# A two-layer transformer kernel: four stages in a row become one pipeline over blocks of 512 queries

## The chip, the cores and the metric

The kernel runs on one core of one Trainium2 chip. The core has a matrix engine (TensorE, PE in the profile; its weight loads are shown as PEld), a vector engine (VectorE, DVE), an activation engine (ScalarE, ACT), a general engine (GpSimd, POOL), and SyncE (SP), which here only issues transfers. Each of them works through its own list of instructions in order. Matrix products are written to PSUM, 8 banks of 512 float32 numbers on each of 128 partitions; everything else lies in SBUF, on 128 partitions, or in DRAM.

The metric is the device time of the whole program in microseconds (us), inputs to output. Three runs are given, and the median counts. The profile is of one further execution.

## The reference, cut to what matters

One sequence of 4,096 tokens with 256 channels goes through two layers, each a modulated norm, a mixer over tokens and a mixer over channels, all in float32 but for the last product.

```python
# sa..gb: six rows of 256 from silu(c) @ wmod; ga, gb pushed away from zero
h = layernorm(x) * (1 + ca) + sa
x = x + ga * attention(h)          # 16 heads of 16, causal softmax; keys gated
h = layernorm(x) * (1 + cb) + sb
x = x + gb * mixture(h)            # shared SwiGLU + 8 experts, the best 2 of a token
# second layer, with its own six rows
h = layernorm(x) * (1 + ca) + sa
x = x + ga * delta_rule(h)         # short convolutions, rotary, chunks of 32, a scan
h = layernorm(x) * (1 + cb) + sb
x = x + gb * quantised(h)          # rounded to int8, 256 x 256 product, rescaled

# attention: out = (softmax(q k / 4, causal) * gate[key]) @ v
#   gate = tanh(g2(gelu(g1(drift)))), drift from a small network on h
# mixture:   wdense = softmax(h @ w_gate) where among the best 2, else 0
#   out = swiglu(h @ w_in) @ w_out + sum_e wdense[:, e] * (swiglu(h @ w1) @ w2[e])
# delta rule, per head and chunk of 32 tokens, k and q normed, beta and gamma gates:
#   T = (I + strict_lower(beta k k'))^-1;  u = T (beta v);  w = T (beta k)
#   u_t = u - w S;  o = q S + tril(q k') u_t;  S = mean(gamma) S + k' u_t
#   core = rmsnorm(o) @ Wo;  plus gate * rmsnorm(sum of dilated shifts of h)
```

Two properties set the order of the work: the attention of a block of 512 queries needs the keys and values of that block and of the earlier ones, none of later ones; and the scan's state S goes through all 128 chunks in order. Mixture, convolutions and the last product work token by token, or look back by at most 8 tokens.

## The kernel before, in words

The kernel runs four stages one after the other, each with its own pools of buffers and banks, each over 8 blocks of 512 tokens.

**Inputs** (`setup`, then `attn_inputs`, from L361): the modulation rows, then for each block the norm (statistics on DVE, the power -1/2 on POOL at L109, the application on DVE at L125), transposes on PE, the products with the weights of k, q and v, and the gate's small network. k and q are stored to DRAM (`kd`, `qd`) as a high and a low half, with rows doubled, so that one product of 48 rows gives the logits at full precision. Values stay in SBUF (`vall`) for all 32 tiles of 128 tokens, multiplied by the gate at the end of the stage.

**Attention** (`interleave`, `maxima`, `weighted`, `divided`): 32 steps, four groups of 4 heads outermost and the 8 query blocks inside, up and down in turn. A step at block T consists of 4T + 3 units: 4T keys tiles before the block, and three for the triangle. For each unit PE makes the logits of 128 keys by 512 queries for 4 heads, as two pairs of heads; the products of a pair lie on different rows of the array, and follow each other with nothing between. Each of those products fills a bank `e` (three banks in turn), and ACT takes the exponential from it at L586. Then PE multiplies by the values into a bank `o`. I call the work with one pair of heads a half-unit; there are 1,088 of them.

The softmax needs its maximum beforehand. `maxima` makes the same logits a second time, the queries in rows: a pair of heads fills a double bank `m` of 1,024 columns (two such in turn), and one DVE reduction over 128 x 2 x 512 takes both maxima, at L479. The negated maximum is stored, as two halves, into two more rows of the query tile by a transfer, so that the product of 50 rows gives logits minus maximum. `maxima` runs up to 4 steps ahead of `weighted`, at a rate worked out from what is due. The full keys of a group (`kts`, 4,096 columns) lie in SBUF in two sets, so that a group's keys are loaded once.

**Mixture** (`mixture`, L626 to L764): per block the output projection, the norm, the choice of experts, two SwiGLU products, and for each tile the shared product and eight experts; DVE adds the experts' products, weighted, into `acc` (L760). All weights lie in SBUF.

**Layer 1** (`layer1`, with two streams, `fronts` and `backs`): the front of a block is its norm, the products for q, k, v, the short convolutions as products with diagonal matrices (`convolve`), transposes (`by_channel`), the products k k' (`products`), and the triangular `solve`, 31 columns of two DVE instructions each (L1194, L1201), whose result goes through DRAM into `U`. The back of a tile is `from_inverse` (u and w), the `scan` of four chunks (PE L146 into bank `w`, DVE `ut` at L1271, PE again, DVE state `S` at L1293), then `weights`, `outputs`, `projected`, and for each block `quantised`. The front runs some 7 pieces ahead; a piece of back and 14/15 of a piece of front follow each other. Four banks `f` serve both.

The order on PE is the order in which the program writes these pieces (`keep_in_program_order` in `mm` and `tp`); DVE's order in layer 1 is fixed for the solve and the scan (`inturn`).

Of the kernel before, what the change touches and what calls it, by code (L numbers as in the profile page):

```python
# [15 lines left out]
PSUM = bass.MemoryType.PSUM  # L16

P = 128
S = 4096
C = 256  # L20
NT = S // P
NB = S // 512
MASKED = -1e30
LN_EPS = 1e-5
V_N = 16 * 17 + 15
AHEAD = 4
HIGH = -4096
ROUND = 12582912.0

K_ID = 0
K_ONE = K_ID + P
K_RANK = K_ONE + 1
K_N = K_RANK + 8
C_QK = 0
C_KQ = C_QK + P
C_N = C_KQ + P
D_INC = 0
D_CH = D_INC + P  # L40
D_EYE = D_CH + 4
D_N = D_EYE + 16 * 32
LEAD = 7
RATE = 14 / 15
KEPT = 8


def _constants():
    import numpy as np

    i = np.arange(P)
    a, b = i[:, None], i[None, :]
    chunk = (a // 32) == (b // 32)

    k = np.zeros((P, K_N), np.float32)
    k[:, K_ID : K_ID + P] = np.eye(P)
    k[:, K_ONE] = (i % 32) == 16
    k[:, K_RANK : K_RANK + 8] = 8 - np.arange(8)
    causal = np.zeros((P, C_N), np.float32)
    causal[:, C_QK : C_QK + P] = np.where(b > a, MASKED, 0.0)  # L60
    causal[:, C_KQ : C_KQ + P] = np.where(a > b, MASKED, 0.0)
    delta = np.zeros((P, D_N), np.float32)
    delta[:, D_INC : D_INC + P] = chunk & (a <= b)
    delta[:, D_CH : D_CH + 4] = ((i[:, None] // 32) == np.arange(4)[None, :]) / 32.0
    eye = np.eye(32, dtype=np.float32)
    for e in range(2):
        delta[64 * e : 64 * e + 64, D_EYE:] = eye[e::2].reshape(1, -1)

    f = np.float32
    freq = f(1.0) / f(10000.0) ** (np.arange(0, 64, 2, dtype=f) / f(64))  # L70
    ang = np.arange(S, dtype=f)[:, None] * freq[None, :]
    trig = np.concatenate([np.cos(ang), np.sin(ang)], axis=1).astype(f)
    return {"const_k": k, "const_causal": causal, "const_delta": delta, "const_trig": trig}


class _Net:
    def __init__(self, ctx, tc, a, out):
        self.ctx, self.tc, self.nc, self.a, self.out = ctx, tc, tc.nc, a, out
        self.n = 0

# [6 lines left out]

    def rows(self, pool, vec, n, tag):

# [5 lines left out]

# [5 lines left out]

# [4 lines left out]
    def power(self, pool, src, n, tag):  # L106

        r = self.t(pool, [P, n], tag)
# [3 lines left out]
    def normed(self, pool, srcs, width, tag):  # L112

        nc = self.nc
        st = self.t(pool, [P, 4, 6], tag + "st")
        mv = self.t(pool, [P, 4, 2], tag + "mv")
# [3 lines left out]
        ve = self.t(pool, [P, 4], tag + "ve")  # L120
        nc.vector.tensor_scalar(ve, mv[:, :, 1], LN_EPS, None, ALU.add)
        rs = self.power(pool, ve, 4, tag + "rs")
        xn = self.t(pool, [P, 4, width], tag + "xn")
        for s in range(4):
            nc.vector.tensor_scalar(  # L125
                xn[:, s, :], srcs[s], mv[:, s, 0:1], rs[:, s : s + 1], ALU.subtract, ALU.mult
# [3 lines left out]
    def transposed(self, psum, tag, src, outs, scale, bias):  # L130

        nc = self.nc
        for k in range(2):
            ps = self.t(psum, [P, 512], tag)
            for s in range(4):
                nc.tensor.transpose(
                    ps[:, s * P : (s + 1) * P], src[:, s, k * P : (k + 1) * P], self.ident
                )
            nc.scalar.activation(
                outs[k], ps, AF.Identity, bias=bias[:, k : k + 1], scale=scale[:, k : k + 1]  # L140
            )

    def mm(self, out, lhsT, rhs, start=True, skip=False):

        self.tc.keep_in_program_order(
            self.nc.tensor.matmul(out, lhsT, rhs, start=start, stop=True, skip_group_check=skip)  # L146
        )
# [3 lines left out]
    def setup(self):  # L151
        nc, a = self.nc, self.a
        self.const = cp = self.ctx.enter_context(self.tc.tile_pool(name="const", bufs=1))
# [6 lines left out]
        nc.vector.memset(self.mhalf, -0.5)  # L160

        with self.tc.tile_pool(name="modw", bufs=2) as wp, self.tc.tile_pool(
            name="modp", bufs=2, space=PSUM
        ) as pp:
            self.mods = [self.modulation(i, wp, pp) for i in range(2)]

    def modulation(self, layer, wp, pp):
# [11 lines left out]

        ps = self.t(pp, [P, 8], "pc")  # L180
        for n, part in enumerate((0, 1, 3, 4)):
            for ch in range(2):
                for k in range(2):
                    nc.tensor.matmul(
# [3 lines left out]
                        start=(k == 0),  # L188
                        stop=(k == 1),
# [3 lines left out]
        for n, name in ((2, "ca"), (6, "cb")):  # L193
            nc.vector.tensor_scalar(col[:, n : n + 2], col[:, n : n + 2], 1.0, None, ALU.add)
        m["sa"], m["ca"], m["sb"], m["cb"] = (col[:, 2 * n : 2 * n + 2] for n in range(4))


        for part, name in ((2, "ga"), (5, "gb"), (3, "sbr"), (4, "cbr")):
# [3 lines left out]
            for k in range(2):  # L202
                nc.tensor.matmul(
                    pr, scb[:, k, :], wm[:, k, part * C : (part + 1) * C], start=(k == 0), stop=(k == 1)
                )
            row = self.t(cp, [P, C], f"{name}{layer}")
# [16 lines left out]

    def attention(self):
        nc, tc, a = self.nc, self.tc, self.a  # L230
        ap_ = self.ctx_attn
        self.vall = self.t(ap_, [P, NT, V_N], "vall")
        self.kts = [[self.t(ap_, [P, S], f"kt{i}{p}", F32R) for p in range(2)] for i in range(2)]
        for pair in self.kts:
            for kt in pair:
                nc.gpsimd.memset(kt.bitcast(F32), 1.0)
        nc.gpsimd.memset(self.vall, 1.0)
        dp = self.ctx.enter_context(tc.tile_pool(name="halves", bufs=1, space=bass.MemoryType.DRAM))
        self.kd = self.t(dp, [3 * C, S], "kd")
        self.qd = self.t(dp, [3 * C, S], "qd")  # L240
        self.attn_inputs()

        wp = ap_
        causal = self.t(wp, [P, C_N], "causal", BF16)
        nc.gpsimd.dma_start(out=causal, in_=a["const_causal"])
        self.masks = []
        for at in (C_QK, C_KQ):
            four = self.t(wp, [P, 4, P], f"mask{at}", BF16)
            nc.vector.tensor_copy(four, causal[:, at : at + P].unsqueeze(1).to_broadcast([P, 4, P]))
            self.masks.append(four)  # L250

        self.mxs = [self.t(wp, [P, 4, 4, 2 + NB], f"mx{i}") for i in range(2)]
        for m in self.mxs:
            nc.gpsimd.memset(m, MASKED)

        with ExitStack() as c:
            e = c.enter_context
            self.qp = e(tc.tile_pool(name="q", bufs=AHEAD))
            self.pexp = e(tc.tile_pool(name="pexp", bufs=10))
            self.small = e(tc.tile_pool(name="asmall", bufs=2))  # L260
            self.ps_e = e(tc.tile_pool(name="ps_e", bufs=3, space=PSUM))
            self.ps_m = e(tc.tile_pool(name="ps_m", bufs=2, space=PSUM))
            self.ps_o = e(tc.tile_pool(name="ps_o", bufs=1, space=PSUM))


            self.interleave([(g, T if g % 2 == 0 else NB - 1 - T) for g in range(4) for T in range(NB)])

    def interleave(self, steps):


        halves = [2 * (4 * T + 3) for _, T in steps]
        start = [sum(halves[:k]) for k in range(len(steps) + 1)]

        order = []
        for k in range(len(steps)):
            order += [(k, False)] * 3 + ([(k - 1, True)] if k else []) + [(k, False)] * (halves[k] - 3)
        order.append((len(steps) - 1, True))
        need = [order.index((k, True)) + 1 for k in range(len(steps))]
        first = [order.index((k, False)) for k in range(len(steps))] + [len(order)]
        streams = {}  # L280
        self.q, done, due = {}, 0, 0.0

        def ahead(upto):
            nonlocal done
            while done < upto:
                k, _ = order[done]
                if k not in streams:
                    streams[k] = self.maxima(*steps[k], k)
                next(streams[k], None)
                done += 1  # L290

        self.load_keys(1)
        for k in range(AHEAD):
            self.load_queries(*steps[k])
        ahead(need[0])
        due, values, tail = float(done), None, None
        for i, (g, T) in enumerate(steps):
            if i and i + AHEAD - 1 < len(steps):
                self.load_queries(*steps[i + AHEAD - 1])
            if i in (9, 17):  # L300
                self.load_keys(g + 1)
            ahead(need[i])
            due = max(due, done)
            limit = first[min(i + AHEAD, len(steps))]
            main = self.weighted(g, T)
            for n in range(halves[i] // 2):
                for half in range(2):
                    made = next(main)
                    at = start[i] + 2 * n + half + 1
                    rates = [  # L310
                        (need[k] - due) / max(start[k] - 4 - at, 1)
                        for k in range(i + 1, min(i + AHEAD, len(steps)))
                    ]
                    due = min(due + max([0.0, *rates]), limit)
# [450 lines left out]

# [700 lines left out]
```

## Time and profile before

| | us |
|---|---|
| three runs | 3,789.13, 3,801.37, 3,807.05 |
| median | 3,801.37 |
| the profiled execution, span | 3,803.7 |
| inputs, from the start to the first weighted unit | 0 to 283 |
| attention | 283 to 2,080 |
| mixture | 2,080 to 2,621 |
| layer 1 | 2,621 to 3,804 |
| busy over the span: PE, PEld | 3,167.0, 1,744.3 |
| busy over the span: DVE, ACT, POOL | 2,234.4, 1,521.2, 451.5 |
| transfers | 88.45 MB, HBM read 51.05, written 33.55 |

The profile gives no time of the execution beside its span. A digit in the 40 slices is the busy share of 95 us in tenths. "Idle before" is how long an engine stood still just ahead of a group's instructions, and the arrow names what ended most of that. A group is one line of the kernel, one operation and one pair of tiles with their shapes (partitions x elements); "x" counts them, and the mean is in ns. A matmul's shape is given as rows of the array by columns of it, then the moving operand; busy matmuls can overlap, so the busy time of PE is that of the union.

### The profile page before, as it was taken

The numbers are of one execution on the slowest core, as the hardware profiler recorded it, in microseconds if no ns is written. First come the engines' busy times: TensorE is split into PE (matmuls) and PEld (weight loads), VectorE is DVE, ScalarE is ACT, GpSimd is POOL, SyncE is SP. The second block draws the span as 40 slices with busy tenths as digits, with TensorE's granted clock in tenths as the row PEclk, the third lists the DMA queues.
The fourth block names the chain that finished last, engine by engine and source line by source line (L and its number), as shares of the span: only waits on it lengthen the run. The fifth ranks groups of instructions, "written<-read, shape, count | busy, mean of one in ns | idle before, by whom it ended". The sixth has DMA issues, their size and how long they took to land. (4 is left out here: it accounts for less than half of the span.)

```text
span 3803.7 us, 52206 instructions
## 1 busy us (share of the span) xinstructions
PE 3167.0 (83%) x20876; PEld 1744.3 (46%) x20876; DVE 2234.4 (59%) x4101; ACT 1521.2 (40%) x3022; POOL 451.5 (12%) x564
## 2 busy tenths in 40 slices
PE   5768899999999899999998898987876887787765
PEld 3444333333334333333334444443755666665644
DVE  4326887877656887877763343444546555554554
ACT  1213565677765565677776111111322122122111
POOL 4230000000000000000000112121312122222211
PEclk7775998999998998999999898987877788878855
DMA  4450000020002000000001100000000000100000
GB/s 131 146 162 10 10 5 5 5 39 5 10 10 52 10 10 5 5 5 5 5 10 40 46 0 1 0 0 23 11 16 14 18 13 14 20 11 15 16 16 12
DMA packets 142563, 88.45 MB, mean 23 GB/s; under 512 B 102448, under 2 KB 120368, under 8 KB 141744
## 3 DMA queue, kind: packets, MB, share of 16 engines
q1 hardware_dynamic: 142176, 85.04, 8.7%
q8 instruction: 165, 2.70, 0.3%
q14 instruction: 78, 0.64, 0.1%
q0 software_dynamic: 144, 0.07, 0.0%
HBM read 51.05 MB, written 33.55 MB: 22 GB/s over the span
## 5 line engine op out<-in xcount | busy, mean ns | idle before, releaser
L479 DVE TENSOR_REDUCE mx<-m 128x2 f32<-128x1024 f32 (+3 forms) x1088 | 1191.4, 1129 | 400.4 <-PE m L146 398.9
L586 ACT ACTIVATE e<-e 128x512 f32<-128x512 f32 (+1 forms) x2176 | 1108.4, 588 | 616.9 <-PE e L146 612.5
L146 PE MATMUL e<-q,kt 50*128 50x512 f32 (+3 forms) x2688 | 731.8, 427 | 106.8 <-ACT e L586 101.4
L146 PEld LDWEIGHTS e<-q,kt 50*128 50x128 f32 x2688 | 326.1, 190 | 749.6 <-ACT e L586 617.9
L146 PE MATMUL m<-kt,q 48*128 48x512 f32 (+2 forms) x2688 | 599.1, 405 | 51.0 <-DVE mx L479 23.5
L146 PE MATMUL o<-e,vall 128*32 128x512 f32 (+3 forms) x5376 | 593.8, 533 | 0.0
L146 PEld LDWEIGHTS m<-kt,q 48*128 48x128 f32 x2688 | 290.1, 198 | 132.4 <-DVE mx L479 64.2
L977 PE MATMUL f<-conv,pT 128*128 128x128 f32 x1536 | 242.9, 313 | 0.0
L667 POOL TENSOR_TENSOR y<-y,ga 128x512 f32<-128x512 f32 x16 | 20.2, 1263 | 1816.1 <-DMA w1s<-in_L_ffn_w_shared_dram 1804.2
L751 PE MATMUL p<-w,hid 128*128 128x512 f32 x512 | 225.0, 592 | 0.0
L977 PEld LDWEIGHTS f<-conv,pT 128*128 128x128 f32 x1536 | 216.1, 220 | 14.2 <-issue 7.0
L146 PEld LDWEIGHTS o<-e,vall 128*32 128x32 f32 x5376 | 118.6, 111 | 172.5 <-issue 167.2
L760 DVE SCALAR_TENSOR_TENSOR acc<-p,wd,acc 128x256 f32<-128x256 f32 x256 | 123.9, 484 | 125.4 <-PE p L751 120.9
L751 PEld LDWEIGHTS p<-w,hid 128*128 128x128 f32 x512 | 97.3, 190 | 108.8 <-issue 107.1
L146 PE MATMUL w<-S,uw 64*32 64x64 f32 x1024 | 64.0, 256 | 97.3 <-DVE S L1293 96.7
L1293 DVE TENSOR_TENSOR S<-gs,w 128x128 f32<-128x128 f32 x128 | 36.3, 283 | 175.5 <-PE w L146 174.6
L487 DVE TENSOR_REDUCE mx<-m 128x8 f32<-128x1024 f32 x64 | 78.5, 1226 | 76.9 <-PE m L146 76.1
L146 PE MATMUL f<-v,U 128*128 128x64 f32 x256 | 45.3, 336 | 68.0 <-DMA U<-dU 67.9
L146 PEld LDWEIGHTS w<-S,uw 64*32 64x32 f32 x1024 | 39.4, 125 | 135.7 <-DVE S L1293 108.7
L977 PE MATMUL f<-frac,hT 128*128 128x128 f32 x640 | 91.2, 297 | 0.0
L747 ACT COPY acc<-p 128x256 f32<-128x256 f32 x32 | 11.9, 373 | 192.9 <-PE p L743 192.9
L977 PEld LDWEIGHTS f<-frac,hT 128*128 128x128 f32 x640 | 84.1, 208 | 3.4 <-issue 0.3
(266 smaller groups left out, 3559.9 us busy)
## 6 DMA issues: line engine op xcount, KB each, us to landing
kd<-half SPq DMA_DIRECT2D x48, 256.0 KB
qd<-half SPq DMA_DIRECT2D x48, 256.0 KB
q<-qd SPq DMA_DIRECT2D x128, 96.0 KB
kt<-kd SPq DMA_DIRECT2D x12, 768.0 KB
x<-in_L_attn_x_dram SPq DMA_DIRECT2D x16, 512.0 KB
Ls<-dL SPq DMA_DIRECT2D x64, 64.0 KB
out_dram<-x SPq DMA_DIRECT2D x8, 512.0 KB
wm<-in_L_wmod_dram SPq DMA_DIRECT2D x2, 1536.0 KB
```

The lines of the kernel that those rows point to most:

```text
L146: self.nc.tensor.matmul(out, lhsT, rhs, start=start, stop=True, skip_group_check=skip)
L479: nc.vector.tensor_reduce(mx[:, 2 * pair : 2 * pair + 2, s, col], ps[:, :, at : at + w], AX.X, ALU.max)
L487: nc.vector.tensor_reduce(mx[:, 2 * pair : 2 * pair + 2, :, 0], ps.rearrange("p h (s k) -> p h s k", k=P), AX.X, ALU.max,)
L586: nc.scalar.activation(e[:, 0:width], ps[:, 0:width], AF.Exp)
L667: nc.gpsimd.tensor_tensor(y, y, m["ga"].unsqueeze(1).to_broadcast([P, 2, C]), ALU.mult)
L747: nc.scalar.copy(acc, ps)
L751: nc.tensor.matmul(ps, hid[1][:, k, rows], w2[:, k, 2 * ep : 2 * ep + 2, :], start=(k == 0), stop=(k == 1),)
L760: nc.vector.scalar_tensor_tensor(acc, ps[:, e2, :], wd[:, s, ei : ei + 1], acc, ALU.mult, ALU.add)
L977: self.nc.tensor.matmul(out, lhsT, rhs, start=(k == 0), stop=(k == n - 1))
L1293: nc.vector.tensor_tensor(self.state, gs, pw[:, 0, 128:256].rearrange("p (a d) -> p a d", d=64), ALU.add)
```

## The change

The four stages become one loop over steps of the attention, now with the query blocks outermost and ascending and the four head groups inside, so that a block's heads are complete after four steps. Three streams run together:

- `attention` gives the order. For each half-unit it makes an e pair, yields a place for one piece of "back" (scan and what follows it), makes the previous unit's values product, makes the next step's maxima, and after every second of these yields a place for one piece of "front". The maxima run one step ahead.
- `fronts` is, in order: the inputs of blocks 0 and 1, the weights of layer 1, then for each block b the inputs of b + 2, and once block b's heads are complete its mixture and its layer 1 front. `step` lets the front advance as long as the PE time that its pieces have taken (estimated in `mm`) is below a due amount, 150 us per 74 units.
- `backs` is the scan and what follows, for 32 tiles.

What is left after the last unit is done in `drain`.

Buffers change with it. PSUM: 2 banks e, 2 single banks m, 1 o, 1 f for the fronts, and one double bank g for the backs; before the first and after the last unit (`solo`) the fronts also use e and m. A pair of maxima products fills two banks m, and two DVE reductions of 128 x 512 take the place of one of 1,024. SBUF: chunks of 512 keys come from DRAM into rings of two, one ring for e and one for m, and values likewise; the heads go to DRAM (`od`) and come back; the weights of the mixture, of q, k, v and of inputs are loaded again for each block. `scr` holds everything short-lived in three sizes, 6 buffers each.

Work is moved between engines, too. `folded` multiplies Wo, the shared output weights and the experts' by ga and gb/2 at the start (on POOL, and stored to DRAM), in place of multiplying results. Silu and sigmoid are written with tanh, with one more DVE operation. The norms are applied on ACT instead of DVE. The solve's 496 instructions go to POOL from DVE; beta is multiplied into L on ACT and into U on POOL, so the transposes of beta k are gone. DVE adds the experts' products straight into x.

```diff
     def attention(self):
+        steps = [(g, T) for T in range(NB) for g in range(G)]
...
+            main = self.weighted(k, steps)
...
+            for n in range(n_units):
+                for half in range(2):
+                    value = next(main)
+                    yield "back", units
+                    if half == 0 and values is not None:
+                        done, values = values(), None
...
+                    want = min(n_max, round(n_max * (2 * n + half + 1) / max(2 * n_units - 3, 1)))
+                    while made < want:
+                        next(ahead, None)
+                        made += 1
+                        if made % 2 == 0 or made == want:
+                            yield "front", units
...
+    def run(self):
+        self.setup()
+        self.resident()
...
+        while self.ready < 1:
+            next(front)
+        self.front, self.back = front, back
+        for kind, units in self.attention():
+            self.step(kind, units)
+        self.solo = True
+        self.drain()
+
+    def step(self, kind, units):
+        if kind == "back":
...
+                self.at = self.advance_back()
+            return
+        due = (units - FIRST) / PER_BLOCK * FRONT_PE
+        if self.spent < due:
+            before = self.pe
+            if next(self.front, self) is self:
+                return
+            self.spent += self.pe - before
...
+            for tag, n in (("e", 2), ("m", 2), ("o", 1), ("f", 1), ("g", 1))
...
     def maxima
-            ps = self.t(self.ps_m, [P, 2, 512], "m")
+            pss = [self.t(self.banks["m"], [P, B], "m") for _ in range(2)]
...
+                    for par, ps in enumerate(pss):
+                        nc.vector.tensor_reduce(mx[:, 2 * pair + par, s, 2 + ch : 3 + ch], ps, AX.X, ALU.max)
...
+    def load_keys(self, z, g, ch):
+        tiles = self.keys[z]
+        kt = tiles[self.loaded[z] % 2]
+        for par in range(2):
+            self.nc.sync.dma_start(
+                out=kt[64 * par : 64 * par + 48].bitcast(F32),
+                in_=self.kd[ch].rearrange("(a b) r n -> b r a n", b=2)[par][:, 2 * g : 2 * g + 2],
+            )
+        v = None
+        if z == "e":
+            v = self.vals[self.loaded[z] % 2]
+            self.nc.sync.dma_start(
+                out=v[:, :, 0:V_N], in_=self.vd[ch][g].rearrange("(j p) n -> p j n", p=P)
+            )
...
     def solve(self, b, later):
-                    nc.vector.tensor_tensor(
+                nc.gpsimd.tensor_tensor(
                     step[:, 0:m, 0:n],
...
-                self.inturn(nc.vector.tensor_tensor(below, below, step[:, 0:m, 0:n], ALU.subtract))
+                nc.gpsimd.tensor_tensor(below, below, step[:, 0:m, 0:n], ALU.subtract)
...
+    def normed(self, srcs, width, tag):
+        rs, nm = self.statistics(srcs, tag)
+        xn = self.scratch([P, 4, width], tag + "xn")
+        for s in range(4):
+            self.nc.scalar.activation(
+                xn[:, s, :], srcs[s], AF.Identity, bias=nm[:, s : s + 1], scale=rs[:, s : s + 1]
+            )
+        return xn
...
+        for src, dst, row in [
+            (a["L0_attn_Wo"], self.wo_d, m["ga"]),
+            (a["L0_ffn_w_shared_out"], self.wso_d, half),
+        ] + [(a["L0_ffn_w2"][i], self.w2_d[i], half) for i in range(8)]:
+            w = self.weight(wp, src, C, "fold")
+            nc.gpsimd.tensor_tensor(w, w, row.unsqueeze(1).to_broadcast([P, 2, C]), ALU.mult)
+            nc.sync.dma_start(out=dst.rearrange("(k p) n -> p k n", p=P), in_=w)
...
+                th = self.scratch([P, B], "th")
+                nc.scalar.activation(th, pa, AF.Tanh, scale=0.5)
+                nc.vector.scalar_tensor_tensor(hh[:, hc, :], th, 1.0, pa, ALU.add, ALU.mult)
...
+    def load_inverse(self, n):
...
+        self.nc.gpsimd.tensor_tensor(
+            U, U, self.tiles[n]["beta"].unsqueeze(2).to_broadcast([P, 4, P]), ALU.mult
+        )
```

## The prediction

> **What bounds the kernel now.** I read the page's totals first, then a table by stretches cut at the four stages, then the attention's waits, groups and timeline, then the last 200 us.
>
> The page, engines and the 40 slices (tenths of a slice busy; PEclk is the granted clock):
> ```profile
> span 3803.7 us, 52206 instructions
> PE 3167.0 (83%) x20876; PEld 1744.3 (46%) x20876; DVE 2234.4 (59%) x4101; ACT 1521.2 (40%) x3022; POOL 451.5 (12%) x564
> ...
> PE   5768899999999899999998898987876887787765
> DVE  4326887877656887877763343444546555554554
> ...
> PEclk7775998999998998999999898987877788878855
> ```
> The stretches: inputs, attention, mixture, layer 1, and layer 1's last part (length, then busy time of PE, weight loads, DVE, ACT, POOL, then the granted clock):
> ```profile
> 0.00:283.00 283.00, 187.74 (x664) 121.09 (x664) 98.73 (x333) 49.99 (x69) 94.62 (x92) 0.75 0.46 147
> 283.00:2080.00 1797.00, 1635.63 (x11376) 673.60 (x11376) 1303.31 (x1308) 1139.14 (x2241) 0.00 (x0) 0.95 0.05 11
> 2080.00:2621.00 541.00, 464.31 (x1281) 248.79 (x1280) 213.72 (x564) 72.29 (x119) 94.64 (x107) 0.88 0.05 15
> 2621.00:3610.00 989.00, 764.65 (x6482) 615.25 (x6483) 519.57 (x1626) 237.03 (x542) 229.88 (x336) 0.81 0.09 16
> 3610.00:3804.00 194.00, 114.70 (x1076) 85.56 (x1074) 99.11 (x273) 22.73 (x52) 32.37 (x31) 0.54 0.06 14
> ```
> PE is the busiest engine of every stage: 66%, 91%, 86%, 77% and 59%. The attention's 161 idle us are few, but the other stages leave 95, 77, 224 and 79 us idle, at lower clocks. So the upper limit of what an overlap can bring is about 640 us of idle PE plus the clock, less what must stay alone at both ends.
>
> Inside the attention, its groups and its waits (busy us, mean ns | idle before it; then who waited for whom, us, times, longest):
> ```profile
> L479 DVE TENSOR_REDUCE mx<-m 128x2 f32<-128x1024 f32 x896 | 1069.3, 1224 | 359.2 <-PE m L146 357.7
> L146 PE MATMUL e<-q,kt 50*128 50x512 f32 x1792 | 613.6, 484 | 92.6 <-ACT e L586 91.3
> L146 PE MATMUL m<-kt,q 48*128 48x512 f32 x1792 | 489.0, 446 | 28.3 <-DVE mx L479 23.5
> ```
> ```profile
> PE e L146 <- ACT e L586: 102.2, 396, 0.5
> ```
> Equal numbers of equal matmuls cost 613.6 us for e and 489.0 for m. The timeline of one unit shows why: with three e banks the second pair of a unit is split, each half running alone after a wait for an exp, where an m pair runs as two in 0.4 to 0.5 us.
> ```profile
> 1801.97 0.50 PE L146 MATMUL e<-q,kt 50*128 50x512 f32 x2
> 1802.31 0.40 PE L146 MATMUL m<-kt,q 48*128 48x512 f32 x2
> 1802.55 0.40 PE L146 MATMUL e<-q,kt 50*128 50x512 f32 x1
> 1803.15 0.50 PE L146 MATMUL e<-q,kt 50*128 50x512 f32 x1 [0.21 <-ACT e L586]
> ```
>
> **The sum is made against the profiled execution**, 3,803.7 us of span with no other time of its own shown; the median of the three runs is 3,801.4, so I treat the two as one. Runs differ by 0.5% (3,789 to 3,807): less than that is "the same", about what a measurement of this kernel can tell from no change.
>
> **The change, part by part.** The new run has three pieces: a head up to the first attention, a pipelined stretch, and a tail for the last block.
>
> *Pipelined stretch, work on PE.* The matmuls stay, but for half of the transposes f<-k,kk (22.2 us), 11. All PE work is then 3,167 - 11 = 3,156. Outside the stretch lie the setup's 25 and one block's inputs (163/8 = 20), and at the end one block's mixture (464/8 = 58), its layer 1 (879/8 = 110) and a third of the scan part of the block before (its rows sum to about 49 a block: 17), by the order in which the changed program's PE instructions stand. That leaves 3,156 - 45 - 185 = 2,926.
>
> *Pairs of e.* Two e banks take the place of three, but between one e pair and the next now stand an m pair, often an o group, and one of 904 inserted pieces of other work of 0.2 to 2.9 us each by their rows. Two exps take 1.2 us (601 ns each). I take e at m's price: -125. Ends: -125 and 0.
>
> *Clock.* The 1,290 us of other work in the stretch ran at 0.75, 0.88 and 0.81 (0.83 weighted); the attention at 0.95. At 0.95 they would take 1,122, a gain of 168; ends 0 and 168. I take 110, because much of layer 1 is small matmuls that keep PE thin wherever they stand. PE work: 2,926 - 125 - 110 = 2,691.
> [...]
>
> *New waits.* The maxima lose their double banks: a pair of m matmuls fills both m banks, and the next pair must wait until both have been reduced. A 128x512 reduce is 685 ns (the row 128x2 from 128x512), so two take 1.37 us where one of 1,024 took 1.22; that adds 0.15 x 896, 130 us in all, to DVE, and the smaller ones some 80. The scan's solve goes to POOL, the apply of three norms to ACT; the tanh forms and fused sums come to DVE. By rows DVE has about 1,500 us of maxima and 850 of other work, 2,370 in all. The stretch has 1,088 half-units (one e pair each): PE 2,691/1,088 = 2.47 us, DVE 1.37 plus (850 - 100)/1,088 = 0.69, 2.06. DVE is below PE, but its queue is in order: the bursts of the convolution's rotation (two of 0.71, two of 0.55, four of 0.35) and its waits for POOL's power (1.0 us) stand between reduces, and behind them the m pair and everything after it on PE. Today PE waits 102 for ACT and 47 for DVE, 0.14 us per half-unit; the other end is that all of DVE's other work shows, 0.69. I take 0.30, nearer to today's since the pieces are spread one to a half-unit: 326 us. The single banks f and g of the inserted work are in it: the next user stands a half-unit or more later, except in two runs of 19 and 21 us for whole inputs.
>
> *The DMA queue.* SP issues 1,667 transfers instead of 816, at 0.3 to 0.56 us, 0.7 ms of its own time, and keys and values are read again for each step: 288 pairs of key loads and 144 of values, some 130 MB. Today's 85 MB took 8.7% of the engines, so about 22%. A chunk is asked for a whole chunk ahead, four units or about 22 us; a 512 KB load issued at 2,089.8 was used at 2,096.9, 7 us later. I cost it at nothing. Were half the chunks 3 us late, it would be 430 us.
>
> *Solve on POOL.* 496 instructions at 0.25 to 0.53 us (the POOL row cs of 128x128 is 530 ns) are 125 to 260 us that the pipeline hides, seven times in eight. POOL and DVE can hold each other up, as these three rows of the last stretch show, where the second of two equal adds takes 3.25 instead of 1.22 us:
> ```profile
> 3715.95 1.22 DVE L1382 TENSOR_TENSOR yxn<-yxn,cbr 128x1024 f32<-128x1024 f32 x1
> 3715.99 3.38 POOL L1396 TENSOR_TENSOR x<-x,bgo 128x1024 f32<-128x1024 f32 x1 [2.38 <-ACT yxn L951]
> 3717.20 3.25 DVE L1383 TENSOR_TENSOR yxn<-yxn,sbr 128x1024 f32<-128x1024 f32 x1
> ```
> POOL did nothing in the whole attention, so no row shows whether reduces suffer too; if each of 250 us of solve held up a reduce, that would be 250 more.
> [...]
>
> *Head.* The first axn stands at 53.7 us today. Before it now come ten weights loaded, multiplied (1.27 us on POOL) and stored through two buffers, five rounds of about 8 us, and the building of 34 diagonal weights on POOL (0.35 us, 12); then the block's chain to its values, 35, and the maxima of the first step. I take 125, ends 95 and 160. The 283 us of today fall away in exchange.
>
> *Tail.* After the last attention unit: a mixture alone, 75 (2,079 to 2,155 today for the first block); layer 1's front for four tiles, 85 (2,650 to 2,735 today); the solve on POOL, 30; from the end of the solve at 3,653.6 to the end today, 150. Sum 340, ends 300 and 390.
>
> **Sum**: 125 + 2,691 + 326 + 340 = 3,482: 3,480 us, 8.5% faster.
>
> **Rivals.** (a) *No better work on PE*: e stays split and the clock low, since two e banks split pairs as three do. 125 + 2,926 + 326 + 340 = 3,717. For it: ACT must return two banks rather than one and a half. Against it: 2.47 us between pairs for 1.2 us of exps.
> (b) *Slower: m pairs wait for DVE.* With one pair of banks PE stands before each m pair until DVE has worked off what stood in front of its reduces. At 0.69 us per half-unit: 125 + 2,691 + 750 + 340 = 3,906. It decides from 0.60 us on, (3,804 - 3,156)/1,088. For it: the tight 2.06 against 2.47 us. Against it: bursts come about 32 times for the convolutions, not 1,088 times.
> (c) *Full overlap*: waits stay at today's 0.14 and the clock reaches 0.95: 125 + 2,633 + 152 + 340 = 3,250.
> That the stages do not overlap at all is excluded by the order on PE: no inserted run but two is over 3.6 us.
>
> **How the numbers follow.** Likeliest (3,330 to 3,640) 50%; (a) and mixtures towards it, up to 3,785, 18%; within 0.5% of before 4%; (b), above 3,823, 24%, since the room on DVE that decides it, 0.41 us a half-unit, is less than one burst; (c) 4%. Faster 0.72, same 0.04, slower 0.24. The range 3,300 to 3,920 takes in (b)'s 3,906, the end of the largest unknown cost, and leaves about 4% below and 10% above.
>
> **What would show it.** Right: PE at 87% or more from 130 us to the last attention unit, granted clock 0.9 or better there, e's busy time near m's, no mixture or layer stretch but the last 340 us, DVE near 2,370 us busy. Wrong: PE waits on mx above 650 us in sum; e or m waiting on key loads; a tail over 400 us; DVE's reduces longer than 0.7 us beside POOL.

## The result, and the profile after

The changed kernel takes 4,580.33 us (median of four runs, 4,568.1 to 4,581.6) against 3,804.21 us (the three runs of before and one more): 1.205 times as long, interval 1.201 to 1.209. The forecast was 3,480 us, faster.

The page of the changed kernel, engines and slices:
```profile
span 4566.3 us, 55163 instructions
PE 3844.8 (84%) x20812; PEld 1912.4 (42%) x20812; DVE 2177.4 (48%) x4732; ACT 1586.6 (35%) x3110; POOL 592.9 (13%) x997
...
PE   3788888898888989888889889988898989888844
DVE  3334453455455545555555545555554555530322
...
PEclk7567897798888878889889868977656985655855
```
About as many matmuls (20,812 for 20,876) keep PE busy for 3,845 us where it was 3,167: PE grew by 678 us, POOL by 141, ACT by 65, and DVE fell. PE's clock is mostly 7 to 9 tenths, where the old attention had 8 or 9 behind its first slice (5), and 5 or 6 in nine of the last twelve slices.

The stretches head, pipeline and tail (cut at the first and behind the last attention unit; length, busy time of PE, weight loads, DVE, ACT, POOL, clock, share of the transfers):
```profile
0.00:127.20 127.20, 52.33 (x198) 35.74 (x198) 48.23 (x104) 12.67 (x22) 48.52 (x76) 0.70 0.56 157
127.20:4222.00 4094.80, 3589.26 (x19335) 1735.41 (x19334) 2024.50 (x4335) 1530.91 (x2990) 472.98 (x807) 0.78 0.24 58
4222.00:4566.30 344.30, 203.27 (x1280) 141.24 (x1280) 104.64 (x293) 42.98 (x99) 71.36 (x114) 0.64 0.08 22
```
Head and tail came as forecast (125 and 340). The pipeline was to take 3,017 us, 2,691 of work and 326 of waits, and took 4,095: 3,589 busy and 506 idle.

Where the work grew, by groups of PE, and who PE waited for longest among them (us in sum, times, longest):
```profile
L165 PE MATMUL m<-km,q 48*128 48x512 f32 x1792 | 670.7, 573 | 141.3 <-DVE mx L655 122.8 <-DVE mx L640 2.5 <-DVE ssq L1193 1.4
L165 PE MATMUL o<-x,v 128*32 128x512 f32 x3584 | 637.3, 792 | 0.0
L165 PE MATMUL e<-q,ke 50*128 50x512 f32 x1792 | 630.5, 569 | 121.9 <-DMA q<-mrow 46.3 <-ACT x L747 38.0 <-issue 36.9
```
```profile
PE m L165 <- DVE mx L655: 122.8, 223, 1.8
PE e L165 <- ACT x L747: 69.2, 106, 3.7
```
The row of o and m's wait in the kernel before (the rows of e and m stand in the prediction):
```profile
L146 PE MATMUL o<-e,vall 128*32 128x512 f32 x3584 | 499.5, 630 | 0.0
PE m L146 <- DVE mx L479: 29.0, 67, 0.9
```
m grew from 489.0 to 670.7 us, e from 613.6 to 630.5, and o, which waits for nobody, from 499.5 to 637.3. The waits themselves are small: the largest is 123 us. So most of the time is not in the waits; each matmul takes longer.

That is the clock, and in places it stays down for long. Three stretches of the changed kernel, and then two of the kernel before:
```profile
3300.00:3440.00 140.00, 127.34 (x414) 44.08 (x414) 73.44 (x120) 50.52 (x93) 0.00 (x0) 0.50 0.18 44
4090.00:4210.00 120.00, 102.17 (x328) 28.00 (x320) 0.00 (x0) 56.61 (x105) 0.00 (x0) 0.50 0.11 27
3520.00:3640.00 120.00, 110.48 (x449) 41.25 (x447) 71.59 (x130) 46.31 (x88) 2.43 (x5) 1.00 0.23 62
```
```profile
1500.00:1530.00 30.00, 30.00 (x112) 10.48 (x114) 17.97 (x15) 13.89 (x27) 0.00 (x0) 0.51 0.00 1
1530.00:1560.00 30.00, 27.35 (x172) 10.18 (x171) 25.90 (x24) 19.22 (x38) 0.00 (x0) 1.00 0.00 1
```
Before, PE at half clock had no gap at all in 30 us (30.00 of 30.00), and had its full clock again behind them. In the changed kernel it is 91% busy for 140 us, and the clock does not come back. The timeline of PE, DVE and ACT in that stretch shows what the 9% are:
```profile
3364.19 0.79 PE L165 MATMUL m<-km,q 48*128 48x512 f32 x2
3364.36 0.34 PEld L165 LDWEIGHTS e<-q,ke 50*128 50x128 f32 x2
3364.79 0.62 PE L165 MATMUL e<-q,ke 50*128 50x512 f32 x2
3365.02 1.29 DVE L655 TENSOR_REDUCE mx<-m 128x1 f32<-128x512 f32 x2 [2.32 <-PE m L165]
3365.45 1.09 ACT L747 ACTIVATE x<-e 128x512 f32<-128x512 f32 x2 [2.32 <-PE e L165]
3365.77 0.28 PEld L165 LDWEIGHTS m<-km,q 48*128 48x128 f32 x1 [1.08 <-DVE mx L655]
3365.77 1.39 PE L165 MATMUL m<-km,q 48*128 48x512 f32 x2 [0.36 <-DVE mx L655]
3366.36 0.28 PEld L165 LDWEIGHTS m<-km,q 48*128 48x128 f32 x1 [0.31 <-DVE mx L655]
```
PE stops for 0.36 us before an m pair, since the two reductions have not left the only two banks m. This wait comes 24 times in the 140 us and makes 10.4 of its 12.7 idle us: with one pair of banks PE and DVE wait for each other in turn. In the second stretch, 4090 to 4210, it is e that waits for ACT, 26 times, all 17.8 us of the idle time.

The clock that both traces record is 1.00 or 0.50 and nothing between (65 spells of each before, 148 of each in the changed kernel; a spell is an unbroken time at one clock). I cut every execution into windows of 1 us and took those with a granted clock below 0.75 as half clock. Of the 147 times at which the changed kernel left half clock, 145 had a run of 3 us without a gap in the 5 us before; of 64 in the kernel before, 57. Of the changed kernel's time at half clock, some 970 us had no such run behind them and saw two returns. So such a run goes ahead of nearly every return, as far as the profile shows PE busy; but it is not enough. The other 1,175 us had one and saw 145 returns, and the first line of the kernel before, above, is 30 us at half clock without a gap.

Nor did the clock come back more slowly on the mean. 147 returns in 2,145 us at half clock are one in 14.6 us; before, 64 in 1,024 are one in 16.0. (Long times at half clock did grow: 16 of over 30 us hold 1,102 of the 2,145 us, where 9 held 442 of the 1,024.) The clock was lost more often: a spell at full clock lasts 16 us on the mean, (4,566 - 2,145)/148, where it lasted 43, (3,804 - 1,024)/65. The spells in both traces are whole multiples of 3.41 us, from 1 upwards (94 of the changed kernel's 296 are one), so I looked at stretches of that length. In the last one before a loss PE stood still for 1.20 us (median, pipeline), in those at full clock with no loss behind them for 0.10 us.

With the same windows any span splits into three: PE's work at full clock (busy time, counted half at half clock), the other half of the busy time at half clock ("lost"), and idle time.

| run (us) | span | full-clock work | lost to half clock | PE idle | us at half clock |
|---|---|---|---|---|---|
| before | 3,804 | 2,813 | 354 | 637 | 1,024 |
| changed | 4,566 | 2,947 | 898 | 721 | 2,145 |

Of the 762 us, 544 are clock, 134 work and 84 idle time. Idle time did not fall, but it is other idle time: the scan's wait for S went from 96.7 to 13.8 us and the last product's for xq from 62.0 to 16.1, while m's for the maxima went from 29.0 to 122.8.

The clock theory, by which the expectations below were written: single waits of about 1 us or less, once a unit, cost little as waits, but they keep PE from the run of 3 us without a gap that stood ahead of 145 of 147 returns (57 of 64 before); and what makes them are the banks that the attention gave up, one pair m for two, and two e for three. That such a run is what brings the clock back is my assumption, and the "only" of the first expectation is more than these counts say. The theory speaks of the return alone; the losses were counted afterwards. The rivals: the pieces of the other stages between the attention's units cost the time; or the clock is a given, and PE's work is the bound.

### The profile page after: what moved, and what is told of

Read it like the earlier page. It is cut to its first block, busy times and chain, and to the rows that moved or that the text cites. A ratio compares the mean times of both kernels' runs of the same rounds, so it can differ in the third digit from the quotient of the medians.

```text
span 4566.3 us, 55163 instructions
## 1 busy us (share of the span) xinstructions
PE 3844.8 (84%) x20812; PEld 1912.4 (42%) x20812; DVE 2177.4 (48%) x4732; ACT 1586.6 (35%) x3110; POOL 592.9 (13%) x997
## 4 chain that ended last, share of the span: by engine, by line
PE 36%; DVE 7%; POOL 3%; issue 3%; ACT 2%; DMA 1%; SPq 0%; POOLq 0%; DVEq 0%; ACTq 0%
PE f L165 9%; PE o L165 9%; PE m L165 7%; PE e L165 5%; PE g L165 4%; DVE mx L655 3%; ACT x L747 1%; POOL step L1255 1%; POOL T L1261 1%; PE f L173 1%; PE g L173 0%; DVE by L1136 0%; DMA q<-mrow 0%; DVE x L994 0%; POOL yxn L1469 0%
## 5 line engine op out<-in xcount | busy, mean ns | idle before, releaser
L747 ACT ACTIVATE x<-e 128x512 f32<-128x512 f32 (+1 forms) x2176 | 1159.1, 583 | 1807.7 <-PE e L165 1781.2
L655 DVE TENSOR_REDUCE mx<-m 128x1 f32<-128x512 f32 x1792 | 1160.8, 685 | 725.4 <-PE m L165 721.2
L165 PE MATMUL m<-km,q 48*128 48x512 f32 (+2 forms) x2688 | 828.3, 520 | 184.8 <-DVE mx L655 122.8
L165 PE MATMUL e<-q,ke 50*128 50x512 f32 (+3 forms) x2688 | 771.8, 500 | 161.8 <-ACT x L747 67.8
L165 PEld LDWEIGHTS m<-km,q 48*128 48x128 f32 x2688 | 371.1, 233 | 963.4 <-DVE mx L655 352.6
L165 PE MATMUL o<-x,v 128*32 128x512 f32 (+3 forms) x5376 | 765.2, 670 | 0.0
L165 PEld LDWEIGHTS e<-q,ke 50*128 50x128 f32 x2688 | 353.3, 226 | 569.8 <-issue 389.8
L165 PE MATMUL f<-w,hid 128*128 128x512 f32 x512 | 267.3, 652 | 12.8 <-DVE x L994 11.0
L640 DVE TENSOR_REDUCE mx<-m 128x1 f32<-128x128 f32 (+2 forms) x384 | 140.4, 416 | 117.8 <-PE m L165 116.8
L165 PE MATMUL f<-hTm,w_in 128*128 128x512 f32 x256 | 144.4, 697 | 9.8 <-DVE hid L955 8.9
```

The lines of the kernel that those rows point to most:

```text
L165: self.nc.tensor.matmul(out, lhsT, rhs, start=start, stop=stop, skip_group_check=skip)
L640: nc.vector.tensor_reduce(mx[:, 2 * pair + par, s, 1:2], ps[:, at : at + P * s], AX.X, ALU.max)
L655: nc.vector.tensor_reduce(mx[:, 2 * pair + par, s, 2 + ch : 3 + ch], ps, AX.X, ALU.max)
L747: nc.scalar.activation(e[:, 0:width], ps[:, 0:width], AF.Exp)
```

## Experiment 1: the attention's banks alone, in the kernel before

```diff
-            self.ps_e = e(tc.tile_pool(name="ps_e", bufs=3, space=PSUM))
-            self.ps_m = e(tc.tile_pool(name="ps_m", bufs=2, space=PSUM))
+            self.ps_e = e(tc.tile_pool(name="ps_e", bufs=2, space=PSUM))   # b_e2, b_e2m1
+            self.ps_m = e(tc.tile_pool(name="ps_m", bufs=1, space=PSUM))   # b_m1, b_e2m1
```
b_e2m1, both:

> The kernel before with one edit: 2 banks e instead of 3 and one double bank m instead of two, as the changed kernel has them; all stages stay in a row. Clock theory (with few banks PE stops for ACT and DVE every unit, also at half clock, so the granted clock, which in both traces comes back only after some 3 us without a gap on PE, stays down): attention from 1,797 to 2,050 or more us, its clock from 0.95 to 0.85 or less, total 4,050 to 4,400. Rival, inserted pieces (the attention is not worse for the banks; the pieces of other stages put between its units cost the time): total 3,800 to 3,900, clock of the attention 0.93 or more.

b_m1:

> The kernel before with one double bank m instead of two, the three banks e kept. Two e and one double m together gave 4,917 us, 1,108 more. If the waits of m for DVE are what keeps PE from a stretch without gaps: 4,300 to 4,750, clock of the attention below 0.8. If it is the e banks: under 3,950.

b_e2:

> The kernel before with two banks e instead of three, both double banks m kept. If m is the cause: 3,850 to 4,150, clock of the attention above 0.85. If e is: 4,300 or more. If each alone costs under 150 us, it takes both to lose the clock.

Both: 4,917 us, 1.290 times before (1.272 to 1.308), more than I expected. m alone: 4,680, 1.229 (1.204 to 1.253), and e alone: 4,114, 1.080 (1.076 to 1.085), both in the ranges for m as the main cause. The attention's stretch of each, as in the tables above, first both, then m, then e:
```profile
283.00:3223.00 2940.00, 2500.75 (x11382) 925.05 (x11382) 1344.12 (x1310) 1190.88 (x2241) 0.21 (x1) 0.63 0.03 7
```
```profile
283.00:2973.00 2690.00, 2202.13 (x11378) 842.87 (x11378) 1342.65 (x1308) 1149.30 (x2241) 0.00 (x0) 0.72 0.03 7
```
```profile
283.00:2391.00 2108.00, 1867.34 (x11387) 729.98 (x11388) 1319.39 (x1310) 1187.45 (x2241) 1.20 (x3) 0.88 0.04 10
```
The attention goes from 1,797 us at a clock of 0.95 to 2,940 at 0.63, 2,690 at 0.72 and 2,108 at 0.88, with no piece of another stage in it. With m's second pair gone, m's wait for DVE is what grew, from 29.0 us:
```profile
PE m L146 <- DVE mx L479: 370.6, 521, 1.5
```
That is b_m1; its spans split into 2,841 of work, 900 lost and 959 idle, both banks together into 2,844, 1,186 and 910: the work is that of before within 1%, and the lost clock is 546 and 832 us more. (b_e2 splits into 2,908, 495 and 706.) Banks alone cost 1,108 us here; the changed kernel with as many banks is 337 us below that. So the pipeline may bring something that its banks take away again; how much is not shown, since the two kernels differ in more than order: one 1,024-wide reduction against two of 512, for one.

What the clock did beside these waits shows in its spells. In the attention's stretch it was lost 61 times in b_m1, 51 with both, 26 in b_e2 and 10 before. A spell at full clock lasted 19, 15, 62 and 146 us on the mean, one at half clock 24, 42, 19 and 18. With the banks gone the clock is above all lost more often, and with both it also comes back later. In b_m1 PE stood still for 1.67 us (median) in the 3.41 us before a loss, and for 0.59 us in such stretches at full clock with no loss behind them. The longest single wait of m for that reduction in this run was 1.5 us (its row above).

## Experiment 2: inputs and attention alone, in the changed kernel

a_attn leaves out mixture, layer 1 and scan:
```diff
-        front, back = self.fronts(), self.backs()
+        front, back = self.fronts(), None
...
             if b + 2 < NB:
                 yield from all_of(self.inputs(b + 2))
-            while self.attended < b + 1:
...
-            yield from all_of(self.mixture(b))
-            yield from all_of(self.layer1(b, later))
...
-        self.drain()
+        for b in range(NB):
+            nc.sync.dma_start(out=self.out.rearrange("o s c -> (o s) c")[B * b : B * b + B, :], in_=self.od[b])
```


> The changed kernel without mixture, layer 1 and scan: inputs and attention alone, heads copied to the output. Its inputs and attention took 2,080 us in the kernel before. Clock theory: 2,300 to 2,700 us with a granted clock below 0.85, spells at 0.50 of 50 us and more with PE 80 to 90% busy. Rival, inserted pieces: 1,950 to 2,100 us at a clock of 0.93 or more, since nothing but inputs is inserted here.

a_attn_m4 has the same, and
```diff
-            for tag, n in (("e", 2), ("m", 2), ("o", 1), ("f", 1), ("g", 1))
+            for tag, n in (("e", 2), ("m", 4), ("o", 1), ("f", 1))
```


> As the run of inputs and attention alone, and 4 banks m instead of 2 (the two of g, which nothing uses here). Clock theory: at least 100 us faster than with 2 banks m, clock higher by 0.04 or more, waits of m for DVE under 60 us. Rival (banks don't matter): within 1% of it.

a_attn_fill has a_attn's banks, and ahead of each m pair
```diff
+            self.filler()    # mm(idle bank g, identb, causal in bf16, 512 columns); nothing reads it
             pss = [self.t(self.banks["m"], [P, B], "m") for _ in range(2)]
```


> The run of inputs and attention alone (3,539 us, clock 0.56), with a product that nothing reads ahead of each m pair: identity by 128x512 in bf16 into a bank of g that is otherwise idle, 0.21 us at full and 0.43 at half clock, 1,100 to 1,200 of them: 230 to 500 us of added PE work. It covers the gaps of 0.2 to 0.4 us in which PE waits for DVE at half clock, and takes no wait away. Clock theory: PE has no gap at half clock, the clock comes back; mean above 0.70, total 2,700 to 3,250. Rival (time is PE's work and waits, the clock is a given): 3,540 to 3,950, clock 0.55 to 0.60.

Measured: 3,539, 2,768 and 3,146 us. Alone the attention is worse than I had said, so the inserted pieces of the other stages are not what slows it: mixture and layer 1 add 1,042 us to this run in the changed kernel (4,580), where they took 1,724 on their own before. (Inputs and attention of b_e2m1, with as many banks, end at 3,223; what makes a_attn slower still, order, loads or the narrower reductions, no run separates.) It is at half clock nearly throughout (a_attn, from 1,000 us to the end):
```profile
1000.00:3534.00 2534.00, 2261.66 (x8510) 796.23 (x8506) 1104.32 (x1852) 960.91 (x1791) 0.00 (x0) 0.52 0.19 46
```
The filler tests whether the clock is a given. It adds work and frees no bank, and the run gets 393 us shorter; its own time covers half of m's waits, which fall from 169.9 to 84.4 us. Its row, and the same stretch (a_attn_fill):
```profile
L165 PE MATMUL g<-causal,identb 128*128 128x512 bf16 x1088 | 481.5, 443 | 0.0
```
```profile
1000.00:3154.00 2154.00, 1927.24 (x9327) 678.92 (x9327) 1096.35 (x1846) 956.83 (x1786) 0.00 (x0) 0.83 0.23 54
```
1,088 products, 482 us as they run, and the clock goes from 0.52 to 0.83. (The expectation had 0.21 and 0.43 us for one. In the kernel before, two such products, `mask` by `identb`, start 0.23 us apart at full and 0.40 at half clock, medians of 115 and 13 pairs.) Full-clock work rises from 1,681 to 2,198 us, and the lost time falls from 1,373 to 553. A clock that is a given cannot do that. Here it is the return that changed: a spell at half clock lasts 62 us on the mean in a_attn and 11 us with the filler. Why is open. Runs of 3 us without a gap lay behind 63% of the time at half clock without the filler and behind 62% with it; runs of 5 us (in the 7 us before) behind 11% and 29%. So longer runs can be the reason, or the product itself, which is 128 x 128 in bf16; a filler of another form was not run. With four banks m the wait itself goes (the sum of m's waits for this reduction falls from 169.9 to 18.3 us), and the lost time is 654; e, still with two banks, then waits 150 us for ACT. m's wait in a_attn, a_attn_fill and a_attn_m4:
```profile
PE m L165 <- DVE mx L657: 169.9, 407, 1.8
PE m L165 <- DVE mx L658: 84.4, 305, 1.2
PE m L165 <- DVE mx L657: 18.3, 58, 0.6
```

## Experiment 3: the banks m in the full mix

a_noback leaves out products, solve, scan and what follows them; a_noback_m4 gives the two free banks g to m, as in experiment 2.
```diff
-        front, back = self.fronts(), self.backs()
+        front, back = self.fronts(), None
...
             later(3, lambda n=n: self.by_channel(n))
-            later(6, lambda n=n: self.products(n, later))
+        nc.sync.dma_start(out=self.out.rearrange(...)[:, 4 * b : 4 * b + 4, :], in_=x4)
```


> The changed kernel without products, solve, scan and what follows them (x is stored after the front of layer 1). It leaves out some 500 us of PE work at full clock and all users of the double bank g. 3,700 to 4,100 us; it is the base for the next run.

> The same without scan, with the two banks of g given to m: 4 banks, two pairs in turn. If single banks m are what opens the gaps in the full mix of attention, inputs, mixture and convolutions too: 250 us or more faster than with 2 banks, clock up by 0.05 or more. If the inserted pieces cover m's waits: within 2% of it.

4,099 and 3,594 us: two banks are worth 504 us in the mix of attention, inputs, mixture and convolutions, too. First a_noback, then a_noback_m4, the wait of m:
```profile
PE m L165 <- DVE mx L655: 138.9, 265, 1.4
```
```profile
PE m L165 <- DVE mx L655: 14.2, 43, 1.2
```
125 us less of waiting, 504 us less of time: lost clock falls from 830 to 467, idle time from 592 to 496, work stays (2,662 and 2,641). The clock rose from 0.77 to 0.85.

## Experiment 4: more work in the changed kernel

a_dup_e computes each unmasked e pair twice:
```diff
+                if not masked:      # the loop over unit and par, as below, start=True
+                    self.mm(ps[:, at : at + w], kt[...], q[...])
                 at = 0
                 for j, lo, w in unit:
```


> The changed kernel, every unmasked e pair computed twice into the same banks: 1,024 pairs more, 0.40 to 0.50 us each at full clock, 410 to 510 us of PE work that nothing needs. Clock theory: the work fills PE's gaps, so the clock comes back more often; mean clock from 0.77 to above 0.80, total 4,450 to 4,800 (-120 to +230). Rival (PE's work is the bound and the clock is a given): +510 to +650, 5,080 to 5,220, clock 0.76 to 0.78.

4,757 us, 177 more. The time is in the range that I gave and well under the rival's, but for another reason: a second pair that follows at once is cheap (e's group holds 895 us for twice the products, where it held 630.5), so that full-clock work rises by 242 us and not by 410 or more. Lost time (900 for 898) and idle time (695 for 721) hardly move, and the clock is 0.777, below the 0.80 that I expected. The added work lies behind the wait for a bank, not in it; m's wait for DVE is still 110 us. This run does not tell the theories apart. The filler, which stands ahead of the wait, does.

## Experiment 5: the values product in two halves

Another way to close gaps is the order. In the changed kernel all four heads' values products stand behind the first e pair of a unit, and the second e pair often comes after an m pair alone. a_osplit puts two heads behind each e pair:
```diff
-                    if half == 0 and values is not None:
-                        done, values = values(), None
+                    if values is not None:
+                        done = values(half)
...
-                for h in range(4):
+                for h in (0, 1) if part == 0 else (2, 3):
```


> The changed kernel with each unit's values product in two halves, two heads behind the first and two behind the second e pair, where all four heads stood behind the first. The second e pair then comes after more than 0.5 us of other PE work. Clock theory: fewer waits of e for ACT, mean clock up by 0.02 or more, 4,300 to 4,530. If only m's waits matter: 4,540 to 4,620.

It took 4,684 us, a miss. (In every fourth unit two heads get the next chunk's values, which are loaded too early for this order.) The clock did rise, to 0.85. The rows tell what it cost:
```profile
L165 PE MATMUL o<-x,v 128*32 128x512 f32 x3584 | 1038.3, 660 | 149.0 <-DMA v<-vd 149.0
```
Each head's product has 32 of the array's 128 columns. At full clock the four products of two heads took 1.05 us here (at 3574.85 us), as long as the eight of four heads in the changed kernel (1.06 us, at 3534.49). So o's 637 us became 1,038, and it waits 154 us for the values. a_osplit2 splits by queries instead, and loads a chunk's values later:
```diff
+            if len(segs) == 1:
+                i, j, lo, w, at = segs[0]
+                h = w // 2
+                segs = [(0, j, lo, h, 0), (1, j, lo + h, h, h)]
+            cut = (len(segs) + 1) // 2
+            return segs[:cut] if part == 0 else segs[cut:]
...
+            if n % 4 == 1 and self.values_due is not None:
+                self.load_values()
```


> The changed kernel with each unit's values product split by queries: 256 columns of all four heads behind the first e pair, 256 behind the second, and a chunk's values loaded one unit later, once the last product with the previous ones is written. The split by heads had a clock of 0.85 against 0.77, but ran two of four column groups (o busy 1,038 us against 637) and waited 154 us for values that it loaded too early. Clock theory: without these two prices 3,950 to 4,350 us, clock 0.82 or more. Rival (the higher clock came from the longer products alone): 4,480 to 4,650, clock under 0.79.

4,609 us, 1.213 times before (1.206 to 1.219), clock 0.755: no gain, within the rival's range; the expectation was wrong. Waiting fell, and the clock did not rise: idle time is 624 us for 721, e's wait for ACT 28, m's for DVE 101, but lost time is 969 for 898. Runs without a gap were not short either: 1,462 of its 2,252 us at half clock had one of 3 us behind them, and one lasted 39 us:
```profile
3964.00:4003.00 39.00, 39.00 (x226) 18.18 (x225) 20.35 (x40) 14.90 (x27) 2.19 (x3) 0.50 0.14 35
```
So gaps alone do not settle the clock. The rival's reading, that the rise in a_osplit came from its longer products, stands; that they cover m's wait is not shown, since it was 90 us there.

b_osplit is the same split in the kernel before, where m has its two pairs:

> The same split in the kernel before, whose values lie in SBUF: no other change. There e waits 102 us for ACT and its pairs are split. If the split closes these gaps: attention from 1,797 to 1,600 to 1,720, total 3,620 to 3,740. If the doubled number of weight loads and products costs as much as it brings: 3,780 to 3,900.

3,658 us, 0.961 of before (0.954 to 0.969): faster than both kernels, and as expected. The attention's stretch and two groups of PE:
```profile
283.00:1936.00 1653.00, 1603.34 (x15220) 742.54 (x15218) 1303.60 (x1312) 1182.42 (x2241) 0.00 (x0) 0.95 0.06 13
```
```profile
L146 PE MATMUL m<-kt,q 48*128 48x512 f32 x1792 | 456.9, 512 | 19.6 <-DVE mx L479 15.6
L146 PE MATMUL e<-q,kt 50*128 50x512 f32 x1792 | 398.7, 421 | 0.0
```
e's pairs are whole now: 399 us where it was 614, with no wait before them. PE is 97% busy in the attention, which takes 1,653 us instead of 1,797; the price is o, whose 7,168 products of 256 columns take 600 us where 3,584 of 512 took 500. This gain is not clock: the profiled span is 151 us shorter, 117 of them idle time, and lost time is 345 us for 354.

## Why the prediction was wrong, step by step

- **Clock, the step that failed**: it took the clock of the attention, 0.95, over to the mix, a gain of 110 us. It was 0.78 in the pipeline: half of the 1,659 us in which PE was busy at half clock there, 829 us, are lost, and over the whole run 544 us more than before are lost where 110 less were forecast. The 0.95 belonged to the old attention with its banks, not to attention work; experiment 1 takes it away with two numbers, and the filler gives much of it back in the attention alone. By which of its waits the full kernel lost it, and what brings it back, stays open. I had looked for a lower limit of this term (0 of 168) and never for a loss.
- **New waits, too low as waits and wrong as a cost**: 326 us forecast, 506 us idle measured in the pipeline. That m would wait for DVE was named, its price taken per wait. b_m1 shows where the larger part is: 322 us more idle, 546 us more lost clock. Rival (b) had the sign and the place, but decided at 0.60 us of waiting per half-unit; the kernel got slower at 506/1,088 = 0.47, waits of all kinds included.
- **Pairs of e**: -125 came, and the clock hides it. e is busy for 630.5 us instead of 613.6, but with its time at half clock counted half, as in the table, it went from 593 to 477 us, 116 less. m went the other way, from 464 to 528, which no term foresaw.
- **DVE**: 2,177 us busy against 2,370 forecast; a 512-wide reduction takes 685 ns as it did in the kernel before. The sum took nothing for a reduction held up beside POOL, which no row of before showed; here the 116 of the 1,792 (L655) that ran beside an instruction of POOL's solve took 686 ns, the others 685, and none over 694. The solve held up no reduction, and the 250 us set beside it were not needed.
- **DMA queue at nothing**: held in the main; 267 MB moved, transfers at 23%, and PE's wait for chunks of keys is some 5 us. What came instead is the wait of an e pair for its stored maximum (q from mrow), 54 us, which I had no term for.
- **Head and tail**: 127 and 344 us for 125 and 340.
- **Upper limit of the gain**: the 637 us of idle PE were to be filled by the overlap. It has 721: the waits of scan and last product were covered, and waits between the attention and its few banks, and for q from mrow, took their place.

A run without a gap went ahead of nearly every return (145 of 147 in the changed kernel behind 3 us of it), but one such run was not enough: 30 us without a gap in the kernel before, and 39 in a_osplit2, stayed at half clock. What was wrong besides was my reading that a stretch with PE at 87% is busy enough for a clock of 0.9; with 91%, and no gap over 0.88 us, the clock stayed at half for 140 us (3300 to 3440).

## What to carry to other kernels

Before you take PSUM banks from a tight loop, ask not only how long PE will wait, but what becomes of its clock. With one pair of banks m in the old kernel it was lost six times as often, behind 1.7 us of standing still in 3.4 (median), and 322 us more of idle time came with 546 us more of lost clock. Of the changed kernel's 147 returns to full clock, 145 had 3 us without a gap ahead of them. A clock measured for one stage was one of that stage's buffers and order: the attention's 0.95 became 0.88, 0.72 and 0.63 with fewer banks and 0.78 in the pipeline, so do not carry it over to a new mix. Where PE waits in short pieces, first move independent work of its own into the gap: the order of one product brought 4% where m kept its two pairs of banks (and nothing where it had one), the pipeline over all stages cost 20%.

## What the hardware showed that I had not expected

- Adding products that nothing reads (482 us as they ran) made a run 393 us shorter, 3,539 to 3,146 us: lost time fell by 820 us, full-clock work rose by 517.
- PE stayed near half clock for a whole stage while 89% busy: clock 0.52 over 2,534 us of a_attn with 2,262 us busy. In the kernel before it stayed there for 30 us with no gap at all (clock 0.51).
- The clock was lost with no long wait: 61 times in b_m1's attention, with 1.67 us of standing still (median) in the 3.41 us before, and no wait of m for its reduction over 1.5 us in the whole run.
- One double bank fewer for the maxima, with the instructions unchanged, made the whole kernel 23% slower; the two bank changes nearly add up, 872 and 305 us apart, 1,108 together.
- The four heads' values products, on 32 columns of the array each, ran at the same time: eight products of four heads took 1.06 us at full clock, four of two heads 1.05, and issuing two heads at a time took 1,038 us instead of 637, at a higher mean clock (0.85 for 0.77).
